# Cross-attention of a decoder layer: where the second score group, the key and value products and the key roots stand

## Chip, cores and metric

The kernel runs on one core of one Trainium2 chip. A core has five engines that each work through their own instructions in order: TensorE (PE, with its weight loads PEld), VectorE (DVE), ScalarE (ACT), GpSimd (POOL) and SyncE (SP, which here only issues transfers). They meet through semaphores. The metric is the device time of one execution in microseconds (us); lower is better. All arithmetic is fp32.

## The reference

One decoder layer over 8 sequences of 112 tokens, width 512: self-attention, cross-attention, and a mixture of experts, each behind a layernorm and added to the residual. The change lies in the cross-attention. Its context has 375 rows for each sequence, and there are 32 heads of 16:

```python
def _L0_xattn_ref(x, context, Wq, Wk, Wv):
    q = x @ Wq.T
    k_raw = context @ Wk.T
    v_raw = context @ Wv.T
    ...
    kv = jnp.concatenate([k_raw, v_raw], axis=-1).reshape(b, m, NHEADS, HEAD_DIM, 2)
    k, v = kv[..., 0].transpose(0, 2, 1, 3), kv[..., 1].transpose(0, 2, 1, 3)
    q = _rmsnorm(q)          # t * rsqrt(mean(t * t) + EPS), over the 16 of a head
    k = _rmsnorm(k)
    attn = jax.nn.softmax(jnp.einsum('bhnd,bhmd->bhnm', q, k) * HEAD_DIM ** -0.5, axis=-1)
    return jnp.einsum('bhnm,bhmd->bhnd', attn, v)   # then heads side by side

x = x + _L0_attn_ref(_layernorm(x, axis=-1), ...)
x = x + _L0_xattn_ref(_layernorm(x, axis=-1), ctx_2048, L0_xattn_Wq, L0_xattn_Wk, L0_xattn_Wv)
x = x + _L0_ffn_ref(_layernorm(x, axis=-1), ...)
```

## The kernel before

The kernel has three stages in a row: self-attention (to about 460 us), cross-attention (to about 760 us) and the experts. In cross-attention the 375 context rows are three tiles (m = 0, 1, 2) of 125 rows, and the 32 heads are two halves (cp = 0, 1) of 16.

The main loop (L674 to L722) runs over the sequences b = 0 to 7 and the two halves of each. A half has three score groups, one for each tile m. `exp_scores` (L569) is one group: 8 products of keys and queries into four PSUM banks (`xs`, pool `sc`, which has just these four), and then four exponentials on ScalarE (L585), one for each bank. A group's products can only be written when the exponentials of the group before have read the banks. When the three groups of a half are done, `pending` holds them, and the next half, behind its own first score group, calls `weigh` (L593) for them: 48 products of exponentials and values (`pv`), and a copy on VectorE (L617). So the weighted values of a half run during the next half.

Between the score groups stands the work that prepares the next sequence, b + 1, and comes in pieces:

- First half, m = 0, 1, 2: one step each of the generator `first_chunks` (L485). It makes keys and values of the context tiles 0 and 1 by a Strassen-like scheme: seven products (`kv`, two instructions each) for eight. Three steps hold two products each; the seventh comes in the second half. The sums of context blocks that it needs (`csum`, `chunk_sums`, L468) are made on GpSimd, for the sequence after that.
- Second half, m = 0: `project_k` (L445), the keys of the third tile (four instructions, `k`), a copy on ScalarE (L446), squares on GpSimd (L412) and their sum over each head on VectorE (L413, `kss`). Then the load of the context of sequence b + 2 is issued, and three of its block sums.
- Second half, m = 1: `project_v` (L449), the values of the third tile (`xv`), copied on VectorE (L450).
- Second half, m = 2: the fourth step of the generator (the seventh product, then an addition on VectorE, L505) and the last block sum (L477).

From sequence 2 on, `attend` (L621) stands behind the second score group of the first half: it transposes and normalises the output of the sequences before (`o_t`) and adds it to the residual. In the last sequence, which has no next one, parts of the experts' stage stand behind groups 1 and 2 (`shared_ahead`, `gu`).

At the end of a sequence's second half come `spread_q` (L536, the queries of the next sequence, on VectorE, L540), `rms_scale` (L416: a square root on ScalarE, L417, and a reciprocal on VectorE, L418, of the key sums `kss`), and `normed_k` (L548). For each of the three tiles that scales the keys on VectorE (L553), transposes them on TensorE (`kT`, 4 instructions a tile, L558) and copies them on ScalarE (L561). The first score group of the next sequence needs the first tile of these.

ScalarE holds the tables of one set of functions at a time. The square root needs another set than the exponential, so there is a table load ahead of it (shown at L417) and another behind it, which the tiny exponential `warm` (L713) brings forward. `tc.issue_after(...)` at L708 makes the roots come behind the exponentials of group m = 1 of the second half; the order that results on ScalarE is exponentials of m = 1, table load, roots, table load, exponentials of m = 2.

In sequence 5, the roots of the third layernorm (L147, `rs3`) are taken at the same place, and four tiles are normalised, transposed and copied behind the keys (`ln_apply`, L156: L153 on VectorE, `ln_t` L160 on TensorE, L161 on ScalarE).

A scheduler orders instructions on each engine. It follows the order of the program largely, but it moves an instruction where its own inputs allow it; on VectorE, for instance, L540 of a sequence stands ahead of where the program has it.

Of the kernel before, what the change touches and what calls it, by code (L numbers as in the profile page):

```python
# [22 lines left out]
B, S, D = 8, 112, 512  # L23
# [53 lines left out]
def decoder_layer(  # L77
# [47 lines left out]
    def load_ctx(b):  # L125
        t = ctxpool.tile([P, ND, M], F32, name=f"ctx{b}", tag="ctx")
        with tc.issue_after(first_weights):
            nc.sync.dma_start(out=t, in_=ctxT[b])
        return t
# [259 lines left out]
    with ExitStack() as xa:  # L389
# [12 lines left out]
        ctxs = {0: load_ctx(0)}  # L402
# [17 lines left out]
        def project(b, m, w, name):  # L420
            ps = psum(mm, name)
            for c in range(ND):
                nc.tensor.matmul(  # L423
                    ps[:MC, :],
                    ctxs[b][:, c, m * MC : (m + 1) * MC],
                    w[:, c, :],
                    start=(c == 0),
                    stop=(c == ND - 1),
                )
            return ps[:MC, :]  # L430

        def by_head(t):
            return t.rearrange("p (h d) -> p h d", h=XH)

        def new_keys(b):
            rawk[b] = (
                krp.tile([MC, NM, 512], F32, tag="kraw", name="kraw"),
                krp.tile([MC, NM, XH], F32, tag="kss", name="kss"),
            )

        def key_squares(b, m):
            k, ss = rawk[b]
            head_squares(MC, k[:, m, :], ss[:, m, :])

        def project_k(b, m):  # L445
            nc.scalar.copy(rawk[b][0][:, m, :], project(b, m, wxk, "k"))  # L446
            key_squares(b, m)

        def project_v(b, m):  # L449
            nc.vector.tensor_copy(values[b % 2][:, m, :, :XD], by_head(project(b, m, wxv, "xv")))  # L450
# [13 lines left out]
        def blocks(b):  # L464
            a = [[ctxs[b][:, 2 * k : 2 * k + 2, m * MC : (m + 1) * MC] for k in range(2)] for m in range(2)]
            return a[0] + a[1]

        def chunk_sums(b, which):  # L468
            a11, a12, a21, a22 = blocks(b)
            sums = (  # L470
                (a21, a22, ALU.add),
                (csum[0], a11, ALU.subtract),
                (a11, a21, ALU.subtract),
                (a12, csum[1], ALU.subtract),
            )
            for i in which:
                nc.gpsimd.tensor_tensor(csum[i], *sums[i])  # L477

        def product(x, w):
            ps = psum(mm, "kv")  # L480
            for c in range(2):
                nc.tensor.matmul(ps[:MC, :], x[:, c, :], w[:, c, :], start=(c == 0), stop=(c == 1))  # L482
            return ps[:MC, :]

        def first_chunks(b):  # L485

            a11, a12, a21, a22 = blocks(b)
            k0, k1 = rawk[b][0][:, 0, :], rawk[b][0][:, 1, :]
            v0, v1 = (values[b % 2][:, m, :, :XD] for m in range(2))
            u = stp.tile([MC, 512], F32, tag="u", name="u")  # L490
            p5 = stp.tile([MC, 512], F32, tag="p5", name="p5")
            nc.scalar.copy(k0, product(a11, wxk[:, 0:2]))
            nc.vector.tensor_tensor(u, product(csum[1], wt[1]), k0, ALU.add)
            yield
            nc.vector.tensor_tensor(k0, product(a12, wxk[:, 2:4]), k0, ALU.add)
            key_squares(b, 0)
            nc.vector.tensor_tensor(k1, product(csum[2], wt[2]), u, ALU.add)
            yield
            nc.scalar.copy(p5, product(csum[0], wt[0]))
            nc.gpsimd.tensor_tensor(v1, by_head(p5), by_head(k1), ALU.add)  # L500
            nc.gpsimd.tensor_tensor(p5, p5, u, ALU.add)
            nc.vector.tensor_tensor(k1, product(a22, wt[3]), k1, ALU.add)
            key_squares(b, 1)
            yield
            nc.vector.tensor_tensor(v0, by_head(product(csum[3], wxv[:, 2:4])), by_head(p5), ALU.add)  # L505
            yield
# [29 lines left out]
        def spread_q(b):  # L536

            queries[b] = qtp.tile([P, ND, 2, S], F32, tag="qT2", name="qT2")
            for e in range(2):
                nc.vector.tensor_scalar(  # L540
                    like_seq(queries[b][:, :, e, :], b),
                    seq(xn2, b),
                    cst[:, C_EO + e : C_EO + e + 1],
                    None,
                    ALU.mult,
                )
# [19 lines left out]
        last_exp = {}  # L566
        warm = stp.tile([1, 1], F32, name="warm")

        def exp_scores(b, cp, m):  # L569


            e = ep.tile([MC, 2, 4, 2, S], F32, tag="e", name="e")
            strips = [psum(sc, f"xs{j}") for j in range(4)]
            for ci in range(2):
                for j in range(4):
                    rows = slice(32 * j, 32 * j + 32)
                    nc.tensor.matmul(  # L577
                        strips[j][:MC, ci * 2 * S : (ci + 1) * 2 * S],
                        keys[b][rows, 2 * cp + ci, m * MC : (m + 1) * MC],
                        queries[b][rows, 2 * cp + ci, :, :],  # L580
                        start=True,
                        stop=True,
                    )
            for j in range(4):
                last_exp[(b, cp, m)] = nc.scalar.activation(  # L585
                    e[:, :, j, :, :].rearrange("p c e s -> p c (e s)"),
                    strips[j][:MC, : 4 * S].rearrange("p (c f) -> p c f", c=2),
                    AF.Exp,
                    scale=float(XD) ** -0.5,
                )  # L590
            return e
# [72 lines left out]
        def shared_ahead(i, k):  # L664


            ps = psum(mm, "gu")
            for c in range(ND):
                nc.tensor.matmul(
                    ps[:, :HALF], sw[0][:, c, i, k, :], xn3[:, c, :HALF], start=(c == 0), stop=(c == ND - 1)  # L670
                )
            nc.vector.tensor_copy(ahead[:, 2 * i + k, :HALF], ps[:, :HALF])

        pending = None  # L674
        for b in range(B):
            for cp in range(2):
                es = []
                for m in range(NM):
                    es.append(exp_scores(b, cp, m))
                    if m == 0 and pending is not None:  # L680
                        weigh(*pending)

                    if m == 1 and cp == 0 and b >= 2:
                        attend(b - 2)
                    if b + 1 < B:
                        if cp == 0:
                            if m == 0:
                                new_keys(b + 1)
                                pairs = first_chunks(b + 1)
                            next(pairs)  # L690
                        elif m == 0:
                            project_k(b + 1, 2)
                            if b + 2 < B:
                                ctxs[b + 2] = load_ctx(b + 2)
                                chunk_sums(b + 2, range(3))
                        elif m == 1:
                            project_v(b + 1, 2)
                        else:
                            next(pairs)
                            if b + 2 < B:  # L700
                                chunk_sums(b + 2, (3,))
                    elif m:
                        shared_ahead(cp, m - 1)
                pending = (b, cp, es)
            if b + 1 < B:
                spread_q(b + 1)

                with tc.issue_after(last_exp[(b, 1, 1)].ins):  # L708
                    if b == 5:
                        rs3 = ln_rstd(mv3, 0, 4)  # L710
                    rms_scale(rawk[b + 1][1].rearrange("p m h -> p (m h)"))

                    tc.keep_in_program_order(nc.scalar.activation(warm, eps_rms[:1], AF.Exp))  # L713
                normed_k(b + 1)
                if b + 2 == B:
                    sw = [load_shared(i) for i in range(2)]
                    ahead = wpool.tile([P, 4, 512], F32, tag="w", name="ahead")
                if b == 5:
                    for t in range(4):
                        ln_apply(mv3, rs3, t, xn3)  # L720
# [7 lines left out]
    with ExitStack() as ff:  # L728
# [363 lines left out]
        pairs = ((0, 4), (1, 5), (2, 6), (3,))  # L1092
# [81 lines left out]
```

## Time and profile before

Three runs took 1018.49, 1020.80 and 1020.93 us (median 1020.8). The profiled execution took 1016.08 us and its span is 1014.3 us. Busy time by stage, from the profile's stretches of the span:

| stretch, us | TensorE busy | VectorE | ScalarE | GpSimd | granted clock | DMA share |
|---|---|---|---|---|---|---|
| 0 to 503.5 | 488.42 | 215.09 | 96.36 | 135.90 | 1.00 | 0.17 |
| 503.5 to 760.5 (scores run) | 255.40 | 93.42 | 135.24 | 65.89 | 1.00 | 0.08 |
| 760.5 to 1014.3 | 247.54 | 93.40 | 45.29 | 44.84 | 1.00 | 0.71 |

How to read the lines that follow below: a group of instructions has its line, engine and operation, then what it writes and from what (`xs<-qT,kT`), and its shape. The count of matmuls in the trace is twice that of the program's instructions (an fp32 product shows as two). In the timeline the two leading numbers are the start and the time from first start to last end; in brackets stands how long the engine had been idle before and what ended that. In the chain, the second number is the share of the chain.

### The profile page before, as it was taken

To read this page: it belongs to the slowest core of one execution; us is meant where nothing else is said; L and a number is where in the kernel's file an instruction comes from. 1 tells how busy PE (TensorE), PEld (TensorE's weight loads), DVE (VectorE), ACT (ScalarE), POOL (GpSimd) and SP (SyncE) were. 2 spreads that over 40 slices of the span, in tenths; PEclk is the share of its full clock that TensorE was granted. 3 is DMA by queue.
4 is the path that set the end of the run, shared out by engine and by line. 5 is a ranking of instruction groups with operands and counts; after the bars stand their busy time and mean duration, and the time that the engine had idled before them with its cause. 6 is when DMAs were issued, how large, how long until landed. Compare 5 with 4: busy or idle time off the path is not lost.

```text
span 1014.3 us, 14761 instructions
## 1 busy us (share of the span) xinstructions
PE 991.4 (98%) x5732; PEld 527.0 (52%) x5732; DVE 401.9 (40%) x769; ACT 276.9 (27%) x522; POOL 246.6 (24%) x269
## 2 busy tenths in 40 slices
PE   5999999999999999999999999999999999999998
PEld 3556555654556455645455555565565544444433
DVE  4345224532345225545432444343425333333315
ACT  2122011310022012213354555455543111221100
POOL 4341034103411122112533223330205600000023
PEclk9999999999999999999999999999999999999999
DMA  9521002101201111000000001000209738777765
GB/s 343 201 83 47 5 38 84 50 1 42 79 16 41 42 41 47 5 1 0 31 32 1 32 32 32 2 32 2 83 3 377 297 112 258 235 235 236 216 190 171
DMA packets 31093, 95.66 MB, mean 94 GB/s; under 512 B 3888, under 2 KB 5808, under 8 KB 27440
## 3 DMA queue, kind: packets, MB, share of 16 engines
q1 hardware_dynamic: 25968, 82.11, 24.0%
q0 software_dynamic: 2320, 7.63, 2.3%
q10 hardware_dynamic: 2736, 4.98, 1.6%
q8 instruction: 46, 0.75, 0.3%
q14 instruction: 23, 0.19, 0.1%
HBM read 78.85 MB, written 14.94 MB: 92 GB/s over the span
## 4 chain that ended last, share of the span: by engine, by line
PE 90%; issue 3%; DVE 3%; DMA 2%; POOL 1%; ACT 1%; SPq 0%; DVEq 0%; POOLq 0%; ACTq 0%
PE qk L261 16%; PE o L348 10%; PE v L338 10%; PE kv L482 9%; PE gu L744 5%; PE xs L577 5%; PE gate L980 4%; PE y L1002 4%; PE up L980 4%; PE pv L602 4%; PE ys L1028 3%; PE k L423 3%; PE xv L423 3%; PE z L226 2%; PE s L191 2%
## 5 line engine op out<-in xcount | busy, mean ns | idle before, releaser
L585 ACT ACTIVATE e<-xs 125x448 f32<-125x448 f32 x192 | 88.4, 545 | 72.7 <-PE xs L577 72.7
L338 PE MATMUL v<-w,xn 128*128 128x512 f32 x224 | 100.4, 594 | 0.0
L348 PE MATMUL o<-wo,zT 128*128 128x512 f32 x224 | 99.8, 594 | 0.0
L261 PE MATMUL qk<-xc,wc 128*128 128x448 f32 x180 | 70.1, 539 | 0.0
L348 PEld LDWEIGHTS o<-wo,zT 128*128 128x128 f32 x224 | 41.0, 190 | 44.0 <-issue 44.0
L338 PEld LDWEIGHTS v<-w,xn 128*128 128x128 f32 x224 | 40.7, 190 | 42.1 <-issue 41.1
L212 POOL TENSOR_TENSOR s<-s,sm 112x448 f32<-112x448 f32 x32 | 30.1, 941 | 129.2 <-DVE sm L211 100.5
L1013 POOL DMA_INDIRECT got<-routed,at x14 | 14.7, 1054 | 173.4 <-DMA routed<-y 169.1
L980 PE MATMUL gate<-wex,xT 128*64 x144 | 55.3, 466 | 0.5 <-ACT xT L945 0.5
L744 PE MATMUL gu<-xn,sw 128*128 128x448 f32 x144 | 55.5, 541 | 0.0
L980 PE MATMUL up<-wex,xT 128*64 x144 | 54.3, 459 | 0.0
L577 PE MATMUL xs<-qT,kT 32*125 32x224 f32 x768 | 50.4, 373 | 1.5 <-DVE qT L540 1.5
L930 DVE COPY xn<-wex 128x704 f32 x60 | 31.2, 524 | 51.5 <-PE up L980 51.5
L261 PEld LDWEIGHTS qk<-xc,wc 128*128 128x128 f32 x180 | 34.2, 190 | 33.4 <-issue 32.3
L261 PE MATMUL qk<-xn,w 128*128 128x448 f32 x120 | 50.2, 539 | 0.0
L577 PEld LDWEIGHTS xs<-qT,kT 32*125 32x125 f32 x768 | 33.2, 181 | 32.5 <-issue 28.5
L1002 PE MATMUL y<-wd,hT 128*64 128x512 f32 (+1 forms) x216 | 49.5, 593 | 0.6 <-ACT y L1006 0.6
L980 PE MATMUL gate<-xn,xT 128*64 128x352 f32 x120 | 45.9, 464 | 0.0
L980 PE MATMUL up<-xn,xT 128*64 128x352 f32 x120 | 45.3, 459 | 0.0
L355 DVE TENSOR_TENSOR x<-o,x 128x512 f32<-128x512 f32 x28 | 19.3, 688 | 62.2 <-PE o L348 62.2
L271 ACT COPY p<-qk 128x448 f32<-128x448 f32 x15 | 8.0, 532 | 126.7 <-PE qk L261 126.7
L208 ACT ACTIVATE s<-s 112x448 f32<-112x448 f32 x32 | 18.5, 577 | 84.3 <-DVE s L207 78.9
(211 smaller groups left out, 1665.4 us busy)
## 6 DMA issues: line engine op xcount, KB each, us to landing
wd<-in_wed_a SPq DMA_DIRECT2D x27, 512.0 KB, 3.8
wex<-in_wegu SPq DMA_DIRECT2D x8, 1408.0 KB, 19.9
wd<-in_wed_b SPq DMA_DIRECT2D x36, 192.0 KB, 4.6
w<-in_wqk SPq DMA_DIRECT2D x6, 1024.0 KB, 4.7
ctx<-in_ctxT SPq DMA_DIRECT2D x8, 750.0 KB, 9.0
slots<-zeros SPq DMA_DIRECT2D x1, 4608.0 KB
wd<-in_wed_a SPq DMA_DIRECT2D x18, 256.0 KB, 4.3
routed<-y SPq DMA_DIRECT2D x18, 256.0 KB, 3.4
```

What stands on the lines that cost most here:

```text
L261: nc.tensor.matmul(ps[:, :HALF], wt[:, c * P : (c + 1) * P], x[:, c, :], start=(c == 0), stop=(c == 1))
L338: nc.tensor.matmul(ps, xn1[:, c, t * P : (t + 1) * P], wv[:, c, :], start=(c == 0), stop=(c == ND - 1))
L348: nc.tensor.matmul(ps, zT[:, h, t * P : (t + 1) * P], wog[:, h, :], start=(h == 0), stop=(h == GH - 1),)
L423: nc.tensor.matmul(ps[:MC, :], ctxs[b][:, c, m * MC : (m + 1) * MC], w[:, c, :], start=(c == 0), stop=(c == ND - 1),)
L482: nc.tensor.matmul(ps[:MC, :], x[:, c, :], w[:, c, :], start=(c == 0), stop=(c == 1))
L577: nc.tensor.matmul(strips[j][:MC, ci * 2 * S : (ci + 1) * 2 * S], keys[b][rows, 2 * cp + ci, m * MC : (m + 1) * MC], queries[b][rows, 2 * ...
L585: last_exp[(b, cp, m)] = nc.scalar.activation(e[:, :, j, :, :].rearrange("p c e s -> p c (e s)"), strips[j][:MC, : 4 * S].rearrange("p (c ...
L602: nc.tensor.matmul(ps[VW * j : VW * (j + 1), g * S : (g + 1) * S], v[:, m, 16 * cp + h, :], es[m][:, h // 8, (h % 8) // 2, h % 2, :], star ...
L744: nc.tensor.matmul(ps[:, :HALF], w[:, c, i % 2, k, :], xn3[:, c, cols], start=(c == 0), stop=(c == ND - 1))
L930: nc.vector.tensor_copy(second(j, c), wex[:, bass.ds(moved[j], 1), c, :].rearrange("p o f -> p (o f)"))
L980: nc.tensor.matmul(gu[k][n, :FF], xT[:, c, n], w, start=(c == 0), stop=(c == ND - 1))
L1002: nc.tensor.matmul(ps[n, :], hT[:fn, i, n], w[i][:fn], start=(i == 0), stop=(i == len(FCH) - 1))
```

## The change

The pieces of preparation get a function, `ahead_of(b, cp, i)`, with the same content for i = 0, 1, 2 as the places m = 0, 1, 2 had. In every half that has a pending one (all but the first half of sequence 0), nothing of it stands behind group 0 any more, piece 0 stands behind group 1, and pieces 1 and 2 stand behind group 2, one after the other. So the order within such a half becomes: scores 0, weighted values, scores 1, (`attend`,) piece 0, scores 2, piece 1, piece 2. The generator of a sequence is kept in a dictionary. The roots at the end of a sequence (and those of the third layernorm in sequence 5) come behind the exponentials of group 2 in place of group 1. The last sequence's order is not changed.

```diff
+        pairs = {}
+
+        def ahead_of(b, cp, i):
+
+            if cp == 0:
+                if i == 0:
+                    new_keys(b + 1)
+                    pairs[b] = first_chunks(b + 1)
+                next(pairs[b])
+            elif i == 0:
+                project_k(b + 1, 2)
+                if b + 2 < B:
+                    ctxs[b + 2] = load_ctx(b + 2)
+                    chunk_sums(b + 2, range(3))
+            elif i == 1:
+                project_v(b + 1, 2)
+            else:
+                next(pairs[b])
+                if b + 2 < B:
+                    chunk_sums(b + 2, (3,))
+
         pending = None
         for b in range(B):
             for cp in range(2):
@@
                     if b + 1 < B:
-                        if cp == 0:
-                            if m == 0:
-                                new_keys(b + 1)
-                                pairs = first_chunks(b + 1)
-                            next(pairs)
-                        elif m == 0:
-                            project_k(b + 1, 2)
-                            if b + 2 < B:
-                                ctxs[b + 2] = load_ctx(b + 2)
-                                chunk_sums(b + 2, range(3))
-                        elif m == 1:
-                            project_v(b + 1, 2)
-                        else:
-                            next(pairs)
-                            if b + 2 < B:
-                                chunk_sums(b + 2, (3,))
+
+
+                        for i in (m,) if pending is None else ((), (0,), (1, 2))[m]:
+                            ahead_of(b, cp, i)
                     elif m:
                         shared_ahead(cp, m - 1)
                 pending = (b, cp, es)
             if b + 1 < B:
                 spread_q(b + 1)
 
-                with tc.issue_after(last_exp[(b, 1, 1)].ins):
+                with tc.issue_after(last_exp[(b, 1, 2)].ins):
```

On the engines the changed program has the order told above on TensorE. On ScalarE the four exponentials of group 2 stand ahead of the table load, the roots and `warm`. On VectorE, L540 stands ahead of the reciprocal L418 in place of behind the scalings L553, and in the first halves the pieces of `attend` (L630, L632, L142, L143) stand ahead of L493; in sequence 5 the addition L505 stands between the second and the third scaling, and two score instructions stand ahead of the last four key transposes on TensorE. On GpSimd and SyncE the order of the instructions is the same.

## The prediction

> **What bounds the kernel now.** I read the page first, for the engines' shares.
>
> ```profile
> span 1014.3 us, 14761 instructions
> PE 991.4 (98%) x5732; PEld 527.0 (52%) x5732; DVE 401.9 (40%) x769; ACT 276.9 (27%) x522; POOL 246.6 (24%) x269
> ```
>
> TensorE has work for 98% of the span. The view of who waited for whom, TensorE alone, cut to cross-attention (503 to 760 us), says how much idle time there is to win:
>
> ```profile
> PE xs L577 <- DVE qT L540: 1.5, 1, 1.5
> PE ln_t L160 <- DVE v L505: 1.1, 1, 1.1
> PE kT L558 <- DVE kraw L553: 0.5, 1, 0.5
> ```
>
> Columns: total us, times, longest. The first wait opens the stage and the change does not touch it. The other two, 1.6 us, stand at the end of sequence 5, the only one that also normalises four tiles for the next stage. So a new order can win the 1.6 us, plus whatever TensorE pays for changing from one kind of product to another. Everything else it can only lose.
>
> Next the chain that ended last, in order of time, for the second half of sequence 3 and for sequence 7:
>
> ```profile
> 616.11 2.44 PE pv L602 x96
> 618.55 3.63 PE k L423 x8
> 622.17 0.97 PE xs L577 x16
> 623.14 3.63 PE xv L423 x8
> 626.77 0.97 PE xs L577 x16
> 627.74 1.91 PE kv L482 x4
> 629.65 1.28 PE kT L558 x12
> 630.93 0.97 PE xs L577 x16
> ...
> 735.05 2.44 PE pv L602 x96
> 737.49 0.97 PE xs L577 x16
> 738.45 1.02 PE o_t L627 x8
> ```
>
> The chain is TensorE without a break: scores (xs) alternate with the products. Sequence 7 already runs the order that the change brings to the others, scores directly behind the weighted values (pv), and both cost there what they cost elsewhere.
>
> Last, the timeline of ScalarE, VectorE and the key transposes in the same stretch (start, duration, engine, line, operation):
>
> ```profile
> 623.22 1.85 ACT L585 ACTIVATE e<-xs 125x448 f32<-125x448 f32 x4 [0.42 <-PE xs L577]
> 625.09 1.28 ACT L417 ACT_TABLE_LOAD   x1
> 626.38 0.37 ACT L417 ACTIVATE kss<-kss,eps_rms 125x96 f32<-125x96 f32 x1
> 626.79 0.75 DVE L418 RECIPROCAL kss<-kss 125x96 f32<-125x96 f32 x1 [2.16 <-ACT kss L417]
> 627.58 0.69 DVE L553 TENSOR_TENSOR kraw<-kraw,kss 125x512 f32<-125x512 f32 x1
> 628.18 0.68 DVE L450 COPY v<-xv 125x512 f32<-125x512 f32 x1
> 628.79 1.28 DVE L553 TENSOR_TENSOR kraw<-kraw,kss 125x512 f32<-125x512 f32 x2
> 629.49 1.45 PE L558 MATMUL kT<-cst,kraw 125*128 125x125 f32 x12
> ```
>
> This is a second chain beside TensorE's: the second group's exponentials, a table load, the roots (L417), a reciprocal, and three scalings of the keys (L553) with a copy (L450) between. It ends at 628.79 + 1.28 = 630.07. The 12 transposes start at 629.49; their last four, a third of 1.28 = 0.43 each, fall due at 629.49 + 0.85 = 630.34. The slack is 0.27 us in 15.8: this is where I looked for the price.
>
> **The change part by part.** *One change of product kind fewer per half.* The timeline starts product pairs after transposes at 606.95 and 608.67 and the next scores at 610.48: 1.72 and 1.81. After pv they start at 601.42, 603.24 and 605.05: 1.82 and 1.81. So a pair costs 1.72 without strange neighbours, and about 0.1 more at each end where scores or pv adjoin. In the new order two pairs touch (first halves), or the value product and a pair (second halves), so two such ends, 0.2 us, go. Scores behind pv cost no extra: 737.42 to 738.38 is 0.96 in sequence 7. This holds in the first halves of sequences 1 to 6 and the second halves of 0 to 6: 13 x 0.2 = 2.6 us won. Sequence 0's first half and sequence 7 are unchanged.
>
> *Second scores behind pv.* They need the four score banks back from the first group's exponentials. In sequence 3 scores start at 615.07, their exponentials run from 616.19 for 1.85 to 618.04, and pv ends at 618.48. The cover is pv's 2.44; 0.44 is left. Without it the scores would wait up to 1.9, but sequence 7 has the order and no wait. Cost 0. The third group follows a 3.63 product, more cover still.
>
> *Moved products and their other work.* VectorE, ScalarE and GpSimd get the same instructions, ordered slightly differently. In second halves the next-but-one queries (L540, 1.23 us) move from behind the scalings to ahead of the reciprocal. They wait for the third scores on TensorE (over at 624.04 in the new order) and stand behind the sum of squares (L413), so they fill time in which VectorE waits for the roots anyhow; uncovered they would cost 1.23. SP's queue keeps its order. The context load that waits for the value product is issued 0.97 later, lands 9.0 us after, near 637, and is first read by GpSimd's L477 near 644. Cost 0; should it be 7 us later, that L477 and the products of the following half would be late. GpSimd's queue keeps its order too: the key squares (L412) start 0.97 later and end by 624.9, their sum by 625.6, ahead of the roots near 627.4. That is 1.8 of cover.
>
> *Roots behind the third group's exponentials.* Counted from the scores at 615.07 with the starts' spacings, TensorE now runs 0.97 + 2.44 + 0.97 + 3.63 = 8.01 to the third scores at 623.08. Before, the roots hung on the second scores at 622.11. The whole chain therefore moves by 0.97, since each link follows its predecessor by the same rows: exponentials over at 626.04, table load to 627.34, roots to 627.7, reciprocal from 627.76, scalings and copy from 628.55, the third scaling over at 631.04. TensorE arrives earlier than before: 623.08 + 0.96 + 3.53 (value product, one end less) + 1.72 (last pair, one end less) = 629.29. The third tile's transposes start 0.15 after their scaling (sequence 5: scalings over at 694.36 + 2.36 = 696.72, transposes at 696.87), at 631.19. The next scores follow after 0.43 + 0.1, at 631.72. Before it was 630.86. Each ordinary change of sequence becomes 0.86 later, its 0.2 already inside: six of them (after 0 to 4 and 6), 5.2 us.
>
> The row for the first link: the table load starts 0.02 after the last exponential (625.09 against 623.22 + 1.85), takes 1.28, and the root starts 0.01 after it. [...]
>
> *Sequence 5.* The same 0.97 for its chain. VectorE's new order there is two scalings, the value addition (L505, 0.61), the third scaling, then the second tile's normalisation. Its three scalings took 2.36, 0.79 each, and begin now at 695.33: two over at 696.90, addition at 697.5, third at 698.3, normalisation at 698.8. The third tile's transposes run 698.44 to 698.87, and the first layernorm transposes at 698.9, before 698.56. But two of the eight score products slip in ahead while VectorE works (0.19). From the first layernorm transposes to pv it was 698.56 to 702.14 = 3.58; now 3.39: pv at 702.3, 0.15 later. The two waits of 1.6 us thus stay.
>
> *Sum.* 6 x 0.86 + 0.15 - 6 x 0.2 (first halves) = +4.1. In five ordinary changes pv waited 0.04 for L505 (2.48 against 2.44 in the chain), which the longer pause swallows: -0.2. In all **+3.9 us**.
>
> *Bounds.* Below: if the third scaling meets its transposes in time, only the 2.6 won remain. Above: if the scalings run at sequence 5's 0.79 instead of the 0.60 spacing (628.18 to 628.79), each chain is 2 x 0.19 to 0.43 later, 6 x 0.43 = 2.6 more: +6.5. I take the ordinary spacing, as five ordinary changes of sequence show it.
>
> The profiled execution took 1016.08 us, 1.8 of it outside the span; with +3.9 it would be 1020.0. The three runs have a median of 1020.8, so the profiled one ran 0.5% quicker than they, and the forecast for a median is 1020.8 + 3.9 = 1024.7.
>
> **The rivals.** *The key chain is in time (not slower).* Place: the third tile's transposes. The change's own gain, 2.6, decides as soon as the third scaling ends by about 630.0, 1.05 us sooner than I count. For it: VectorE is idle before the reciprocal, and the copy (L450) could have been done ahead of it. Against: the copy stands behind the first scaling in VectorE's order, and the chain's links are all rows of this trace. 1020.8 - 2.6 = 1018.2.
>
> *The pause of sequence 5 goes as well (faster).* Queries ahead of the reciprocal free VectorE 0.8 there; were that to clear both waits, it would be -2.6 - 1.6 = -4.2: 1016.6. Against: the roots of that sequence start 0.97 later.
>
> *VectorE and GpSimd slow each other (slower still).* The last partial sum of the context (GpSimd L477, 0.87) now begins about 629.4, beside the second scaling. At the 0.79 rate it is +6.5: 1027.3. For it: sequence 5 shows 2.36 for three with such a sum beside them. Against: sequence 3 has the sum beside its third scaling and two took 1.28.
>
> **How the numbers follow.** Forecast (+1.5 to +6 us) 0.68; key chain in time 0.17; sequence 5 clears too 0.05; slowed scalings 0.10. About 0.3%, 3.1 us, is what a measurement of this kernel can tell from no change. Of the forecast's 0.68 some 0.50 lies above +3.1, the rest below. Slower: 0.50 + 0.10 = 0.60. Same: 0.18 + 0.17 = 0.35. Faster: 0.05. The range runs from 1019.5 (the forecast's low side with a median 1 us off, as the runs scatter from 1018.49 to 1020.93) to 1027.5 (slowed scalings); outside lie the larger part of the in-time case, the faster case and tails, under 0.2.
>
> **What would show it.** Right: a wait of TensorE's kT transposes for L553 in every change of sequence, summing to 4 to 6 us; chain rows of joined products with 0.2 less (first halves 7.05 for two pairs instead of 2 x 3.63); scores behind pv still 0.97; the table load of L417 0.02 behind the third exponentials; sequence period 33.5 instead of 32.9. Wrong: no such wait; a wait of the second scores for the exponentials; a context load or L477 that the products wait for; sequence 5 with pv more than 0.5 from my time.

## The result, and the profile after

| | before | changed |
|---|---|---|
| median of 9 runs, us | 1018.13 (1015.67 to 1020.93) | 1023.56 (1021.19 to 1026.05) |
| ratio to before | | 1.005, 95% interval 1.0034 to 1.0066 |
| span of the profiled execution, us | 1014.3 | 1024.3 |
| first score product to the start of the last weighted values, us | 254.86 | 262.22 |

The change makes the kernel slower by 0.5%, some 5.4 us. The spans of the two profiles differ by 10.0, but not all of that is the change: the first score product starts at 503.47 in the one and 505.88 in the other, 2.4 us apart, before any instruction that the change moves. So the stretch in the last row is compared below, and it is taken from the timeline of TensorE in each profile: from the first start of `xs` to the last start of `pv`. The two starts before, and the two in the changed kernel:

```profile
503.47 1.04 PE L577 MATMUL xs<-qT,kT 32*125 32x224 f32 x16 [1.47 <-DVE qT L540]
...
758.33 2.51 PE L602 MATMUL pv<-e,v 125*32 125x112 f32 x96
```

```profile
505.88 1.04 PE L577 MATMUL xs<-qT,kT 32*125 32x224 f32 x16 [1.47 <-DVE qT L540]
...
768.10 2.51 PE L602 MATMUL pv<-e,v 125*32 125x112 f32 x96
```

The page of the changed kernel, its first two lines:

```profile
span 1024.3 us, 14768 instructions
PE 996.0 (97%) x5732; PEld 530.2 (52%) x5732; DVE 401.5 (39%) x769; ACT 279.5 (27%) x522; POOL 247.2 (24%) x269
```

TensorE has the same 5732 products and is idle for longer. The waits of TensorE during cross-attention in the changed kernel (total us, times, longest) say where:

```profile
PE kT L558 <- DVE kraw L553: 6.1, 6, 1.4
PE xs L577 <- DVE qT L540: 1.5, 1, 1.5
PE kT L558 <- ACT kT L561: 0.6, 1, 0.6
```

The opening wait is as before. The key transposes now wait in every one of the seven changes of sequence, six times by this table for the scalings; the seventh, behind sequence 6, is put down to ScalarE's copy of the first tile. The timeline there shows both candidates:

```profile
741.80 1.28 DVE L553 TENSOR_TENSOR kraw<-kraw,kss 125x512 f32<-125x512 f32 x2
742.02 0.58 ACT L561 COPY kT<-kT 128x500 f32<-128x500 f32 x1 [0.74 <-PE kT L558]
742.62 1.22 PE L558 MATMUL kT<-cst,kraw 125*128 125x125 f32 x8 [0.64 <-ACT kT L561]
```

The first of the two scalings, which is the second tile's, ends near 741.80 + 0.68 = 742.48 and the copy at 742.60, so the profile names the copy. The transposes stand 0.14 behind the scaling here, as they do in sequence 3, where the copy had ended 0.35 before them; and in the kernel with early roots (below) the second tile's transposes are under way before the copy of the first tile starts. They need the scaling, not the copy. The wait of sequence 5's layernorm transposes for L505, 1.1 before, is not in the table any more. The chain that ended last, for the second half of sequence 3, to be set beside the one before:

```profile
621.37 2.44 PE pv L602 x96
623.81 0.97 PE xs L577 x16
624.77 3.63 PE k L423 x8
628.40 1.05 PE xs L577 x16
629.45 1.85 ACT e L585 x4
631.32 1.28 ACT L417
632.61 0.38 ACT kss L417
633.02 0.76 DVE kss L418
633.78 0.02 issue
633.80 0.69 DVE kraw L553
634.50 0.60 DVE v L450
635.10 0.93 DVE kraw L553
636.02 0.14 issue
636.16 1.22 PE kT L558 x8
637.38 0.97 PE xs L577 x16
```

Before, this was TensorE from end to end. Now it leaves TensorE at the third scores and comes back at the transposes: exponentials, table load, roots, reciprocal, scaling, copy, scaling. The value product and the last pair of TensorE lie beside it and decide nothing.

### The profile page after: what moved, and what is told of

Same layout as the page of the kernel before. It is cut to its first block, busy times and chain, and to the rows that moved or that the text cites. A ratio compares the mean times of both kernels' runs of the same rounds, so it can differ in the third digit from the quotient of the medians.

```text
span 1024.3 us, 14768 instructions
## 1 busy us (share of the span) xinstructions
PE 996.0 (97%) x5732; PEld 530.2 (52%) x5732; DVE 401.5 (39%) x769; ACT 279.5 (27%) x522; POOL 247.2 (24%) x269
## 4 chain that ended last, share of the span: by engine, by line
PE 87%; DVE 4%; issue 3%; ACT 2%; DMA 2%; POOL 1%; SPq 0%; DVEq 0%; POOLq 0%; ACTq 0%
PE qk L261 15%; PE o L348 9%; PE v L338 9%; PE kv L482 7%; PE xs L577 5%; PE gu L753 5%; PE gate L989 4%; PE y L1011 4%; PE up L989 4%; PE pv L602 4%; PE ys L1037 3%; PE k L423 3%; PE z L226 2%; PE s L191 2%; PE qk L316 1%
## 5 line engine op out<-in xcount | busy, mean ns | idle before, releaser
L412 POOL TENSOR_TENSOR sq<-kraw 125x512 f32<-125x512 f32 x24 | 25.1, 1046 | 86.8 <-ACT kraw L446 44.1
```

## The experiments

The whole-kernel times scatter by several us, so the steps between the starts of weighted values are the measure. "Inside" is the step from a sequence's first half to its second (sequences 2 to 4), "over" the one across a change of sequence (after 1 to 4), then the one after 5, with its layernorm, and the one after 6.

| kernel | inside | over | after 5 | after 6 | stretch |
|---|---|---|---|---|---|
| before | 17.05 | 15.83 | 20.33 | 15.79 | 254.86 |
| changed | 16.86 | 16.97 | 22.27 | 16.66 | 262.22 |
| changed, second profile | 16.86 | 16.98 | 20.65 | 16.66 | 260.61 |
| roots behind group 1 again | 16.86 | 15.59 | 18.56 | 15.60 | 250.69 |
| old order, roots late | 17.4 to 18.7 | 21.6 to 22.4 | 27.12 | 22.05 | 305.95 |
| first halves alone | 16.86 | 15.83 | 20.34 | 15.79 | 253.97 |
| second halves and late roots alone | 17.05 | 16.98 | 20.65 | 16.66 | 261.78 |
| last context sum left out | 16.86 | 16.66 | 20.13 | 16.66 | 258.52 |
| value copy on ScalarE | 16.86 | 16.54 | 19.35 | 16.06 | 256.54 |

**Roots behind group 1 again**, all else as changed:

```diff
-                with tc.issue_after(last_exp[(b, 1, 2)].ins):
+                with tc.issue_after(last_exp[(b, 1, 1)].ins):
```

> The changed order of score groups and products, but the roots behind group 1's exponentials again, so that on ScalarE they stand ahead of group 2's. Measure: the stretch from the first score product to the start of the last weighted values (254.9 us in the kernel before, 262.2 in the changed one), and the step from one start of weighted values to the next that spans a change of sequence (15.83 before, 16.97 changed). Theory K (the key chain is late because the roots hang on the third exponentials): the roots then wait only for the sum of the key squares, about 1.7 us earlier, all scalings are over before their transposes, TensorE waits nowhere for L553, the step is 15.6 and the stretch about 252, 3 us under the kernel before; whole time 0.3% under it. Rival P (the new places of scores and products cost the time themselves, whatever the roots do): the step stays near 17.0 and the stretch near 262. Rival E (late second exponentials of group 2, now behind two table loads, hold up the next scores): the step lies between, and scores wait for L585.

It took 1012.88 us (median of 6, 1010.87 to 1013.41) against 1018.10 for the kernel before: 0.9941, interval 0.9918 to 0.9963. The timeline of this kernel over the same change of sequence:

```profile
623.55 1.28 ACT L417 ACT_TABLE_LOAD   x1
...
625.40 0.38 ACT L417 ACTIVATE kss<-kss,eps_rms 125x96 f32<-125x96 f32 x1 [0.57 <-DVE kss L413]
625.79 1.28 ACT L585 ACT_TABLE_LOAD   x1
...
626.79 1.89 DVE L553 TENSOR_TENSOR kraw<-kraw,kss 125x512 f32<-125x512 f32 x3
627.09 1.85 ACT L585 ACTIVATE e<-xs 125x448 f32<-125x448 f32 x4
...
628.60 0.69 DVE L450 COPY v<-xv 125x512 f32<-125x512 f32 x1
...
629.06 1.45 PE L558 MATMUL kT<-cst,kraw 125*128 125x125 f32 x12
...
629.69 1.54 ACT L561 COPY kT<-kT 128x500 f32<-128x500 f32 x3 [0.70 <-PE kT L558]
```

And all that TensorE waits for between 503 and 760 us:

```profile
PE xs L577 <- DVE qT L540: 1.5, 1, 1.5
```

The roots now wait for the sum of the key squares (L413) and not for exponentials. The three scalings end at 626.79 + 1.89 = 628.68, before the transposes start at 629.06, and the copy L450 falls behind them. Group 2's exponentials pay for it, behind two table loads, and end at 628.94; the next scores start at 630.43, so nothing waits for them. The step that theory K put at 15.6 is 15.59, and both rivals fall: no wait is left but the one that opens the stage, so the places of scores and products cost nothing. The stretch is 1.3 us shorter than expected, because sequence 5 gained 1.8 as well: its pauses went, which had not been in the sum. The second tile's transposes begin about 0.43 behind the first tile's, at 629.49, while the first copy starts at 629.69: they do not wait for it.

**Old order, roots late**, the opposite part alone:

```diff
-                with tc.issue_after(last_exp[(b, 1, 1)].ins):
+                with tc.issue_after(last_exp[(b, 1, 2)].ins):
```

> The order of before on TensorE, only the roots moved behind group 2's exponentials. Theory K: group 2's scores stand at 11.6 us in the half, so the roots come some 4.6 us later than in the kernel before; the third scaling ends about 3.8 us after its transposes are due. The step over a change of sequence is 15.83 + 3.8 = 19.6, six of them 23 us, sequence 5 about 3.6 more: stretch 281 to 282. If pauses of 3 us also lower TensorE's granted clock for a while, up to 1.7 us more in each: to 293. Rival P (places cost, roots don't): stretch 255, step 15.83.

The 1.7 us for a pause is an estimate; the changed kernel's windows behind sequence 5 (below) lose 1.70 us of clock.

1068.46 us, once. The direction is K's and P falls, but the stretch is 306.0 where K had at most 293. The waits of this kernel's transposes, all seven, and its stretches of 5 us around one change of sequence, then the whole of cross-attention (after the window and its length: busy us with counts of PE, PEld, DVE, ACT and POOL, then granted clock, DMA share, GB/s):

```profile
PE kT L558 <- DVE kraw L553: 23.3, 7, 3.7
```

```profile
650.00:655.00 5.00, 2.14 (x12) 0.67 (x4) 2.60 (x5) 4.65 (x7) 0.67 (x1) 1.00 0.46 154
655.00:660.00 5.00, 4.59 (x22) 3.17 (x25) 1.56 (x3) 2.08 (x5) 0.00 (x0) 0.60 0.00 0
660.00:665.00 5.00, 5.00 (x108) 4.00 (x102) 0.61 (x1) 1.96 (x4) 0.00 (x0) 0.72 0.02 3
665.00:670.00 5.00, 5.00 (x32) 2.75 (x31) 1.14 (x4) 1.66 (x4) 0.00 (x0) 1.00 0.01 2
```

```profile
503.00:815.00 312.00, 286.88 (x2803) 164.21 (x2802) 96.08 (x171) 139.78 (x268) 66.73 (x80) 0.92 0.07 23
```

The waits themselves are 3.3 us in the mean, near the 3.8 expected. What was mis-sized is the clock: behind the pause it stands at 0.60 and then 0.72 of full speed, and with 5 x 0.40 + 5 x 0.28 = 3.4 us of lost clock in these ten, a pause of 3.3 us costs by this estimate about twice its length; the steps over a change, 21.6 to 22.4, are 5.8 to 6.6 longer than before. Over the whole stretch the mean clock is 0.92, some 25 us lost in 312; with 23.3 of waits that is most of the 51.1 by which the stretch is longer.

**The two halves apart.** First halves alone, with the roots at group 1:

```diff
-                        for i in (m,) if pending is None else ((), (0,), (1, 2))[m]:
+                        for i in (m,) if pending is None or cp else ((), (0,), (1, 2))[m]:
...
-                with tc.issue_after(last_exp[(b, 1, 2)].ins):
+                with tc.issue_after(last_exp[(b, 1, 1)].ins):
```

Second halves alone, with the roots at group 2:

```diff
-                        for i in (m,) if pending is None else ((), (0,), (1, 2))[m]:
+                        for i in ((), (0,), (1, 2))[m] if cp else (m,):
```

> The new order in the first halves alone, second halves and roots as in the kernel before. Theory K with the saving of 0.2 us for each end of a product kind that goes: six first halves (sequences 1 to 6) give 0.2 each, the step inside a sequence falls from 17.05 to 16.86, over a change it stays 15.8; stretch 254.9 - 1.2 = 253.7. Rival P: the first halves cost as much as the second ones, step 17.05 + 0.5 or more, stretch 258 or more.

> The new order and the late roots in the second halves alone, first halves as in the kernel before. Theory K: the whole loss of the change is here, and the first halves' saving is missing: step over a change of sequence 16.97, inside a sequence 17.05, stretch 262.2 + 1.2 = 263.4. Rival P (the loss is spread over both kinds of halves): stretch about 258 to 259.

First halves alone: inside 16.86, over 15.83, stretch 253.97 for 253.7 expected (1015.49 us once). One step over a change was 16.11, the others 15.8, which is the 0.3 missing; its cause is open. Second halves alone: over 16.98, inside 17.05, stretch 261.78 (1024.43 us once). Expected was 263.4, counted from a stretch with the lowered clock of sequence 5, which did not come here; without it the sum is 261.8. So the first halves win their 0.2 each and the whole loss is in the second halves with their late roots.

**The changed kernel again**, unedited:

> The changed kernel itself, once more, to see what of its profile repeats. Theory K: the steps over a change of sequence repeat to 0.02 (16.97 five times, 16.66 once). Theory C (the drop of TensorE's granted clock behind sequence 5, to 0.50 for some 3 us, depends on where the pause falls and not on the program alone): sequence 5 takes 22.27 with the drop and 20.65 without, as in the run with second halves alone; either may come. If the drop belongs to the program, it comes again at the same place.

All steps repeat to 0.01 but one: after sequence 5 it is 20.65, not 22.27. The windows of the first profile of the changed kernel there:

```profile
700.00:704.00 4.00, 2.65 (x9) 1.02 (x8) 3.36 (x6) 2.31 (x5) 0.67 (x1) 1.00 0.00 0
704.00:706.00 2.00, 1.95 (x14) 1.23 (x13) 1.93 (x4) 1.16 (x2) 0.00 (x0) 0.92 0.00 0
706.00:708.00 2.00, 2.00 (x12) 2.00 (x10) 0.41 (x1) 0.99 (x2) 0.00 (x0) 0.50 0.00 0
708.00:710.00 2.00, 2.00 (x11) 1.24 (x10) 0.68 (x2) 0.81 (x3) 0.00 (x0) 0.73 0.00 0
```

In the second profile the clock is 1.00 in the same four, after the same pause:

```profile
700.00:704.00 4.00, 2.64 (x9) 0.98 (x7) 3.63 (x7) 2.05 (x4) 0.67 (x1) 1.00 0.00 0
704.00:706.00 2.00, 1.95 (x15) 1.36 (x15) 1.66 (x4) 1.16 (x2) 0.00 (x0) 1.00 0.00 0
706.00:708.00 2.00, 2.00 (x16) 1.55 (x15) 1.00 (x2) 1.55 (x3) 0.00 (x0) 1.00 0.00 0
708.00:710.00 2.00, 2.00 (x43) 1.54 (x44) 0.00 (x0) 1.93 (x4) 0.00 (x0) 1.00 0.04 8
```

The three windows with the drop lose 2 x 0.08 + 2 x 0.50 + 2 x 0.27 = 1.70 us of clock. Taken in windows of 0.25 us it is 0.50 in each from 705.75 to 709.00, 0.85 in the one before and 0.83 in the one behind: half speed for some 3.4 us. The drop costs 22.27 - 20.65 = 1.6 us and is a matter of the run. Without it the change costs 260.61 - 254.86 = 5.75 in the profile, beside 5.4 by the medians. In the timed runs it can only be read from the mean granted clock of each: of the nine of the changed kernel five show 0.997 or 0.998 (1022.68 to 1026.05 us) and four 0.999 or 1.00 (1021.19 to 1023.56), so a lowered clock seems to come in about half of them, though where is not recorded. The kernel before has it too: of the 11 runs taken beside the experiments three show 0.996 or 0.997 (1020.86 to 1021.50) and eight 0.999 or 1.00 (1015.77 to 1018.76). So a part of the scatter, on both sides of the 5.4, is the clock.

**The last context sum.** One edit placed it elsewhere in the program:

```diff
             if cp == 0:
                 if i == 0:
+                    if b:
+                        with tc.issue_after(last_exp[(b, 0, 1)].ins):
+                            chunk_sums(b + 1, (3,))
                     new_keys(b + 1)
...
                 next(pairs[b])
-                if b + 2 < B:
-                    chunk_sums(b + 2, (3,))
```

> The changed kernel with GpSimd's last partial sum of the context (L477) taken out of the change of sequence and put behind group 1's exponentials of the next half. Theory S (that sum, running beside the scalings, makes two of them take 1.60 us in place of 1.28): sequences 0 to 4 lose the surplus and step over a change in 16.65, as sequence 6 does, which has no such sum; stretch from first score product to last weighted values 262.2 - 5 x 0.32 = 260.6, or 259.0 if TensorE's granted clock does not drop behind sequence 5. Rival (the scalings are slow for another reason, or the wait is bound elsewhere): step 16.97 as before.

It did not move: GpSimd has nothing else to do there, so the sum ran where it had run, beside the scalings, and every step is that of the second profile of the changed kernel (stretch 260.61). Placing it after an instruction of ScalarE did not make GpSimd wait here: in sequence 3 L477 starts at 633.74 after 4.65 of idle time, and the two scalings from 633.96 take 1.60 as in the changed kernel. So the sum was left out instead (that edit's deletion alone):

> The changed kernel without GpSimd's last partial sum of the context (L477 at the end of a second half); the sum is left out for the contexts of sequences 2 to 7, so their values of the first tile are computed from an old sum. The run with the sum placed later did not test this, since GpSimd's order had nothing else to put ahead of it and the sum ran where it had run. Theory S: in the changes after sequences 0 to 4 the two scalings take 1.28 in place of 1.60 and the step over a change is 16.65 in place of 16.97, as after sequence 6; sequence 5 falls from 20.65 to about 20.3; stretch 260.6 - 1.9 = 258.7. Rival: step 16.97, scalings 1.60.

Over 16.66, after 5 20.13, stretch 258.52. The timeline shows both cases, first in the changed kernel (one scaling, then the sum), then with the sum left out (two scalings):

```profile
634.80 0.67 POOL L477 TENSOR_TENSOR csum<-ctx,csum 128x250 f32<-128x250 f32 x1 [4.66 <-PE kv L482]
```

```profile
635.01 1.00 DVE L553 TENSOR_TENSOR kraw<-kraw,kss 125x512 f32<-125x512 f32 x1
```

```profile
631.93 1.28 DVE L553 TENSOR_TENSOR kraw<-kraw,kss 125x512 f32<-125x512 f32 x2
```

The second scaling takes 1.00 beside the sum, against 0.68 undisturbed (1.28 for two with starts 0.60 apart), and the 0.32 reaches the sequence whole: 16.97 against 16.66.

**Value copy on ScalarE**, out of VectorE's key chain:

```diff
-                project_v(b + 1, 2)
+                nc.scalar.copy(values[(b + 1) % 2][:, 2, :, :XD], by_head(project(b + 1, 2, wxv, "xv")))
```

> The changed kernel with the copy of the third tile's values (L450, 0.60 us between the first and the second scaling) moved from VectorE to ScalarE, behind the roots. Theory K (each 0.1 us on VectorE's key chain is 0.1 us of the sequence): the second and third scaling come 0.60 earlier, the step over a change falls from 16.97 to 16.37, in sequence 6 from 16.66 to 16.06; stretch 262.2 - 6 x 0.6 = 258.6, or 257.0 without a drop of the clock. Rival (the transposes wait for the copies on ScalarE or for banks, not for the scalings): the step stays, or grows by the copy's 0.6.

After 6, where no sum runs, 16.06 as expected: 0.60 off the chain is 0.60 off the step. Over the other changes 16.54 for 16.37, because the sum still meets a scaling:

```profile
631.89 2.38 DVE L553 TENSOR_TENSOR kraw<-kraw,kss 125x512 f32<-125x512 f32 x3
...
632.88 0.84 POOL L477 TENSOR_TENSOR csum<-ctx,csum 128x250 f32<-128x250 f32 x1 [4.65 <-PE kv L482]
```

Three took 2.38, where they take 1.89 undisturbed. The stretch of 256.54 (1019.19 us once, beside 1015.59 before) recovers 4.1 of the 5.75; it is still longer than that of the kernel before.

## Why the prediction was right, and where it was off

The forecast was +3.9 us, slower, 1024.7; measured are +5.4 and 1023.56, with the median of before lower in the longer series than in the first three runs. That the time came within 1.1 us is partly luck: the base was 2.7 too high and the change 1.5 too small, and the two errors have opposite signs. The change itself, 5.4, lies nearer to the 6.5 of the rival with slowed scalings than to the 3.9. The lower end of the range does not follow from its own words either: 1020.8 + 1.5 - 1 is 1021.3, not 1019.5; the measured time lies above both. By its own steps, against the second profile of the changed kernel:

- *One change of product kind fewer*: 0.2 for each half. Measured 17.05 to 16.86 inside, 0.19, and the same with first halves alone. Right.
- *Second scores behind pv, free*: right. The early-roots kernel has this place in the same halves, and no score group waits there.
- *Moved products, copies, queries, loads, free*: right by the same kernel; what was left out was that a scaling is longer beside the sum that moved (1.00 in sequence 3, 0.68 undisturbed).
- *Roots late*: 0.86 for an ordinary change, all of it in the wait of the transposes (6.1 + 0.6 = 6.7 in the table, sequence 5 with it, above the 4 to 6 named as a sign). The prediction put the wait at the third tile; most of it, 0.96 in sequence 3, now stands ahead of the second. Where nothing disturbs the scalings it is 16.66 - 15.79 = 0.87. Where the context sum runs it is 16.98 - 15.83 = 1.15. The term that was mis-sized is the spacing of the scalings: "I take the ordinary spacing". It came out at 1.60 for two in place of 1.28, in five of the six ordinary changes, 1.6 us together. The rival with slow scalings had named that sum, at a larger price (0.43 a change; measured 0.32), and was put aside with a row read too lightly: in the kernel before the sum came behind the start of a scaling, and it was the sum that took longer (0.87 there, 0.67 now; its row stands below the list). In both kernels it is the one that started second that took longer, and the change turned their order.
- *Sequence 5*: +0.15, measured +0.32 with the clock at full speed. That its two waits of 1.6 us stay was wrong, though the total hardly moves: the layernorm transposes' wait for L505 went, and the key transposes' wait grew from 0.5 to 1.35, now ahead of the first tiles. The sum on GpSimd has its part here as well: with it left out the step is 20.13, under the 20.33 of before. A lowered clock behind the longer pause was not in any case of the prediction; it added 1.6 in one profile of two, and there pv of sequence 5 is 1.9 later, beyond the 0.5 that the prediction had named as a sign of being wrong.

The last context sum in the kernel before, in the same change of sequence as the rows of the prediction:

```profile
629.73 0.87 POOL L477 TENSOR_TENSOR csum<-ctx,csum 128x250 f32<-128x250 f32 x1 [5.82 <-PE kv L482]
```

Sum of the measured terms: five ordinary changes at 1.15, one at 0.87, sequence 5 at 0.32, six first halves at -0.19: 5.75 + 0.87 + 0.32 - 1.14 = 5.8, the 5.75 of the stretch.

The prediction's row for the table load came again: in the changed kernel the exponentials are over at 629.45 + 1.85 = 631.30, the load starts at 631.32, takes 1.28, and the root starts at 632.61. In both profiles such a load stands ahead of the roots and another behind them in all seven changes of sequence.

Beside each other, the sum and a scaling: in the changed kernel the sum ends at 635.47, 0.46 behind the second scaling's start at 635.01, and the scaling takes 0.32 longer; before, 0.34 of the scaling were left when the sum started (630.07 - 629.73), and the sum took 0.20 longer. Why one is longer beside the other no run shows. In the early-roots kernel the sum (629.30 to 629.97) runs beside the addition L505 (from 629.26), and both keep their times, 0.67 and 0.69.

## What to carry to other kernels

With TensorE busy for 98% of the span, joining products of one kind saved little but surely here (0.2 us at each seam), and what it costs is decided by the chain of small instructions beside it: before moving a root or a reduction behind a later instruction, count its chain to the consumer, since here 0.27 us of slack (0.12, if the 0.15 from a scaling to its transposes is counted) was spent by a move of 0.97. The two halves of such a change are worth trying apart: the new order with the roots left early is faster than either kernel (0.9941). And if an elementwise instruction of another engine is moved beside that chain, ask which of the two starts first: here the one that started second took 0.20 or 0.32 us longer.

## What the runs showed of the hardware that was not expected

TensorE's granted clock fell in one profile behind a pause of little more than 1 us, and not in another: in the first profile of the changed kernel TensorE was idle for 1.35 us, then ran 8 transposes and 4 score instructions of the trace, and the clock went to 0.50 for some 3.4 us (1.00 at 705.25 to 705.50, 0.50 from 705.75 to 709.00, 1.00 from 709.25); in the second profile it stayed at 1.00 behind a pause of 1.36 us in the same place, and so it did behind 1.35 us in the run with second halves alone. In the old order with late roots, whose pauses are 3.3 us in the mean, the clock over the 10 us behind one of them was 0.66 in the mean (0.60, then 0.72), and 0.92 over the whole stretch. What decides whether it falls, and for how long, no run here shows.
